# Layer 2's tail and layer 3's tables in six staged groups, degrees broadcast from DRAM, and one loop for long rows instead of three

## The chip, the core and the metric

The kernel runs on one core of one Trainium2 chip. The metric is the device time in microseconds (us). The engines of a core work independently: TensorE (PE; its weight loads are PEld in the profile), VectorE (DVE), ScalarE (ACT), GpSimd (POOL) and SyncE (SP). SP only issues DMAs here. DMAs move data between the core's memory (SBUF) and DRAM.

## The reference

Four graph layers are applied one after the other to x (2708 nodes with 128 features each). The adjacency matrix `adj` is 2708 x 2708; it is sparse (about four entries off the diagonal per row, plus the diagonal). Each layer normalises its input per node, takes its positive part, and adds its result to x.

```python
h = relu(layernorm(x)); x = x + L0(h, adj)   # normalised adjacency @ (h W + b)
h = relu(layernorm(x)); x = x + L1(h, adj)   # attention, 128 groups, adj added to the logits
h = relu(layernorm(x)); x = x + L2(h, adj)
h = relu(layernorm(x)); x = x + L3(h, adj)

def L2(f, adj):
    deg = adj.sum(axis=1, keepdims=True)
    deg = where(deg == 0, 1, deg)
    agg = adj.T @ f / deg
    h = agg @ W_n.T + b_n + f @ W_c.T + b_c
    mu, var = h.mean(axis=0), ((h - h.mean(axis=0)) ** 2).mean(axis=0)
    return relu(gamma * (h - mu) * rsqrt(var + 1e-5) + beta)

def L3(f, adj):
    a, b = f @ w1[:, :128].T, f @ w1[:, 128:].T
    gi = sigmoid(a[None] + b[:, None] + b1) * adj[:, :, None]
    return einsum('ijf,jg->ig', gi, f) @ weight + bias
```

Layer 3 needs, for a node i and each neighbour j, the rows a[j] and f[j]; for the node itself it needs b[i] + b1, and x[i] for the final addition.

## The kernel before

**Tiles.** Nodes lie on the 128 partitions in 22 row tiles (21 full ones and one of 20 rows). Products over all nodes have six column groups of 512 (the last has 148), so a column group is four row tiles. All data are float32. The running x is `x_sb` in SBUF.

**Layer 0** reads the adjacency twice and builds, per node, a sorted list of up to 16 neighbours. It leaves the row sums in `deg` (128 x 22). **Layer 1** takes most of the time; its order of work is written out by hand, and the change does not touch its code. It ends with the last addition to `x_sb` at line 691.

**Layer 2** begins at L1454:

- SP loads the two weights, and these are transposed (L203 to L218). SP loads four columns (L200): two biases, gamma and beta.
- `di`, the inverse degree, is computed on VectorE (L1475 to L1477). It is needed along the free dimension, the same on all partitions (`diB`, 128 x 2708). 22 times, VectorE scales the identity by a column of `di` (L1481), TensorE multiplies a matrix of ones with it (L1483), and ScalarE copies the product to `diB` (L1484).
- SP issues the loads of adjacency row tiles (L1462) into four buffers.
- Two loops (L1498, L1551) stand for inputs on which layer 1's short form is not accurate. Their counts are zero with these inputs, so they are skipped, but all engines take part in the skip, and SP's part waits for the transfers issued earlier.
- `norm_relu` (L220 to L249) makes h and its transpose. The sums (L1578) run over row tiles, six matmuls each, into six banks of PSUM. They are multiplied with `diB` (L1583), put through two linear maps (L1591, L1594), biased (L1597), and VectorE gathers the statistics of the batch norm (L1598 to L1603).
- Per column group, y is normalised on VectorE (L1606), scaled and made positive on ScalarE (L1607), transposed back tile by tile (L1611), and added to `x_sb` (L1612).

**Layer 3** begins at L1617:

- SP loads `w3`, `b3`, `b1` and `w1`. GpSimd clears `more` (L1626). `norm_relu` runs over all 22 tiles: all statistics, one square root (L231), all normalisations (L234, L238), then the transposes (L245, L248).
- Per row tile, TensorE makes a and b together (L1634) and adds b1 through a matmul with a row of ones (L1641). ScalarE copies a (L1645) and h (L1646) into `tab`; VectorE copies b + b1 into `bn` (L1647); SP stores `tab` into the table `gate_d` in DRAM (L1648): one row of 256 values per node, and a row of zeros at the end (L1651).
- Three loops (L1688, L1708, L1752) stand for rows with more neighbours than the lists hold: a count, the rounds, and the addition of `more`. Their counts are zero here. A short computation between the first and the second (L1698 to L1706) yields the number of rounds.
- SP stores `own_d` (b + b1 and x per node) by two calls of `store_rows` (L185 to L189), after these loops in its queue for the second half.
- Per row tile, GpSimd gathers the tile's own rows (L1783) and its neighbours' rows (L1657, 121 gathers in all) by indirect DMAs. The other engines work out the gated sum and the last linear map (L1664 to L1799). GpSimd scatters the result to the output (L1770).

The order within this part comes from the order of the program; each engine works through its own queue in order, and SP's queue holds all the loads and stores above.

Of the kernel before, what the change touches and what calls it, by code (L numbers as in the profile page):

```python
# [9 lines left out]
FP = mybir.dt.float32  # L10
# [6 lines left out]
P = 128  # L17
# [28 lines left out]
def gnn4_kernel(  # L46
# [474 lines left out]


# [929 lines left out]

    with ExitStack() as ph:
# [11 lines left out]
        with tc.tile_pool(name="l2_ps0", bufs=2, space=PSUM) as ps:  # L1465
            wnT = transposed(lp, wk_pool, ps, wn2, "wnT")
            wcT = transposed(lp, wk_pool, ps, wc2, "wcT")
            bias = column_of(lp, bn2, "bn2_sb")
            bc_sb = column_of(lp, bc2, "bc2_sb")
            g_sb = column_of(lp, gamma, "g_sb")  # L1470
            be_sb = column_of(lp, beta, "be_sb")
            nc.vector.tensor_tensor(bias, bias, bc_sb, ALU.add)

            di = lp.tile([P, NT], FP, name="di")
            nc.vector.tensor_scalar(di, deg, 0.0, None, ALU.is_equal)  # L1475
            nc.vector.tensor_tensor(di, di, deg, ALU.add)
            nc.vector.reciprocal(di, di)  # L1477
            diB = lp.tile([P, N], FP, name="diB")
            for t, (r0, sz) in enumerate(rows):
                dg = lp.tile([P, P], FP, name="dg", tag="dg", bufs=2)  # L1480
                nc.vector.tensor_scalar_mul(dg[:sz, :sz], ident[:sz, :sz], di[:sz, t : t + 1])  # L1481
                pd = ps.tile([P, BK], FP, name="d_ps", tag="tr")
                nc.tensor.matmul(pd[:, :sz], ones[:sz], dg[:sz, :sz], start=True, stop=True)  # L1483
                nc.scalar.copy(diB[:, r0 : r0 + sz], pd[:, :sz])  # L1484
# [119 lines left out]
        for c, (c0, cw) in enumerate(cols):  # L1604
            yc = y[:, c0 : c0 + cw]
            nc.vector.tensor_scalar(yc, yc, mv[:, 0:1], rstd, ALU.subtract, ALU.mult)  # L1606
            nc.scalar.activation(yc, yc, AF.Relu, bias=be_sb, scale=g_sb)  # L1607
            for t, (r0, sz) in enumerate(rows):
                if c0 <= r0 < c0 + cw:
                    pt = ps.tile([P, BK], FP, name="y_tr", tag="tr")  # L1610
                    nc.tensor.transpose(pt[:sz, :C], y[:, r0 : r0 + sz], ident)  # L1611
                    nc.vector.tensor_tensor(x_sb[:sz, t], x_sb[:sz, t], pt[:sz, :C], ALU.add)  # L1612


    gate_d = dram.tile([N + 1, 2 * C], FP, name="gate_d")
    own_d = dram.tile([N, 2 * C], FP, name="own_d")
    with ExitStack() as ph:  # L1617
        lp = ph.enter_context(tc.tile_pool(name="l3", bufs=1))
        w3_sb = lp.tile([C, C], FP, name="w3_sb")
        nc.sync.dma_start(w3_sb, w3)  # L1620
        b3_sb = row_of(lp, b3, "b3_sb")
        b1_sb = row_of(lp, b1, "b1_sb")

        bn = lp.tile([P, NT, C], FP, name="bn")
        more = lp.tile([P, NT, C], FP, name="more")
        nc.gpsimd.memset(more, 0.0)  # L1626
        with tc.tile_pool(name="l3w", bufs=1) as wk_pool, tc.tile_pool(
            name="l3_pw", bufs=4, space=PSUM
        ) as ps, tc.tile_pool(name="l3_tab", bufs=4) as tp:
            w1T = transposed(lp, wk_pool, ps, w1, "w1T")  # L1630
            h, hT = norm_relu(lp, ps, "3")
            for t, (r0, sz) in enumerate(rows):
                pw = ps.tile([P, BK], FP, name="ab_ps", tag="tr")
                nc.tensor.matmul(  # L1634
                    pw[:sz, : 2 * C],
                    hT[:, r0 : r0 + sz],
                    w1T.rearrange("p a c -> p (a c)"),
                    start=True,
                    stop=False,
                )  # L1640
                nc.tensor.matmul(  # L1641
                    pw[:sz, C : 2 * C], ones[0:1, :sz], b1_sb, start=False, stop=True
                )
                g = tp.tile([P, 2, C], FP, name="tab")
                nc.scalar.copy(g[:sz, 0], pw[:sz, :C])  # L1645
                nc.scalar.copy(g[:sz, 1], h[:sz, t])  # L1646
                nc.vector.tensor_copy(bn[:sz, t], pw[:sz, C : 2 * C])  # L1647
                nc.sync.dma_start(gate_d[r0 : r0 + sz], g[:sz].rearrange("p a c -> p (a c)"))  # L1648
            z = tp.tile([1, 2 * C], FP, name="tab_z")
            nc.vector.memset(z, 0.0)  # L1650
            nc.sync.dma_start(gate_d[N : N + 1], z)  # L1651
# [27 lines left out]
        with tc.tile_pool(name="l3_more", bufs=2) as mp, tc.tile_pool(  # L1679
# [5 lines left out]
            nc.vector.memset(last, float(N + 1))  # L1685
            nc.vector.memset(count, 0.0)
            adj_flat = adj.rearrange("n m -> (n m)").rearrange("(e o) -> e o", o=1)
            with tc.For_i(0, nc.values_load(ovf, min_val=0, max_val=1)):  # L1688
                ri = mp.tile([P, N], I32, name="key")
# [7 lines left out]
            most = mp.tile([P, 1], FP, name="most")  # L1697
            nc.vector.tensor_reduce(most, count, axis=AX.X, op=ALU.max)  # L1698
            pt = ps.tile([P, BK], FP, name="most_ps", tag="most_ps")
# [139 lines left out]
```

## Time and profile before

| What | us |
|---|---|
| Time before, median of 3 runs | 3235.08 (3232.13 to 3238.72) |
| The profiled execution | 3207.61 |
| Its span, first to last instruction | 3205.8 |
| POOL busy in the span | 2003.3 |
| PE busy | 2615.1 |
| Layer 1's last addition to `x_sb` | begins 2745.79 |
| First matmul of layer 2's sums | begins 2776.29 |
| Batch norm's reciprocal | begins 2892.56 |
| First matmul of layer 3's tables | begins 2920.50 |
| First gather of layer 3 | begins 2979.57 |

A line of the timeline reads: start, time, engine, line of the kernel, operation, output <- inputs, how many in a row, and in brackets the idle time before and what ended it. In the page, a row of digits gives 40 equal slices of the span (9 is 90% busy or more); PEclk is the granted clock of TensorE in tenths.

### The profile page before, as it was taken

How to read it: one execution, taken by the hardware profiler on the slowest of the kernel's cores; microseconds unless marked ns; L12 is line 12 of the kernel's file. 1: busy time of each engine (PE TensorE's matmuls, PEld its weight loads, DVE VectorE, ACT ScalarE, POOL GpSimd, SP SyncE). 2: the span in 40 equal slices, each digit the busy share in tenths (PEclk: the TensorE clock that was granted, in tenths of full speed). 3: DMA queues.
4: the chain of work that ended last, by engine and by line, in shares of the span. 5: the costliest groups of instructions: out<-in, count | busy, mean ns of one | idle time of the engine just before them, and what ended most of it. 6: DMA issues, size and time to landing. Idle time of an engine off the chain costs nothing. (4 is left out here: it accounts for less than half of the span.)

```text
span 3205.8 us, 50411 instructions
## 1 busy us (share of the span) xinstructions
PE 2615.1 (82%) x17997; PEld 2222.6 (69%) x17997; DVE 2182.9 (68%) x5130; ACT 1300.2 (41%) x3165; POOL 2003.3 (62%) x2264
## 2 busy tenths in 40 slices
PE   6477895888889999999999999999888888697144
PEld 4376644887888888878878887878788887443133
DVE  3868744777778888888888887888777676304222
ACT  3576333666644444444444444444433333102010
POOL 0212115666688888888998898989767664000676
PEclk6699897999999999999999999999989999795565
DMA  3463174787733333333343333343355543451332
GB/s 107 175 228 124 66 325 158 238 243 238 210 134 116 131 118 129 137 127 138 118 146 134 138 133 132 137 146 133 84 149 137 125 119 94 165 217 51 102 93 75
DMA packets 309523, 462.53 MB, mean 144 GB/s; under 512 B 153774, under 2 KB 229488, under 8 KB 284178
## 3 DMA queue, kind: packets, MB, share of 16 engines
q1 hardware_dynamic: 277658, 290.28, 28.4%
q0 software_dynamic: 31600, 168.86, 15.4%
q8 instruction: 149, 2.44, 0.3%
q14 instruction: 116, 0.95, 0.1%
HBM read 344.49 MB, written 114.59 MB: 143 GB/s over the span
## 5 line engine op out<-in xcount | busy, mean ns | idle before, releaser
L1302 PE MATMUL g_ps<-mw,fT 128*128 128x128 f32 x5632 | 795.7, 283 | 146.2 <-ACT fT L1292 99.1
L1302 PEld LDWEIGHTS g_ps<-mw,fT 128*128 128x128 f32 x5632 | 707.7, 194 | 265.9 <-ACT fT L1292 155.6
L1292 ACT COPY fT<-f_ps 128x512 f32<-128x512 f32 (+1 forms) x768 | 419.8, 547 | 1114.0 <-PE f_ps L1290 1113.3
L1264 PE MATMUL m_ps<-y,fk 123*128 123x128 f32 (+1 forms) x5632 | 740.0, 276 | 0.0
L1264 PEld LDWEIGHTS m_ps<-y,fk 123*128 123x128 f32 (+1 forms) x5632 | 686.5, 193 | 0.0
L1212 POOL TENSOR_TENSOR y<-bk,raw 128x792 f32<-128x792 f32 x256 | 415.3, 1623 | 386.9 <-ACT y L1245 381.4
L1310 DVE TENSOR_TENSOR z<-g_ps,bq 128x324 f32<-128x324 f32 (+1 forms) x768 | 354.3, 461 | 350.7 <-PE g_ps L1302 350.5
L1290 PE MATMUL f_ps<-ident,fq 128*128 128x128 f32 x2816 | 438.0, 275 | 14.4 <-DVE fq L1209 4.7
L1316 DVE TENSOR_REDUCE o_raw<-z 128x36 f32<-128x324 f32 (+1 forms) x768 | 355.7, 463 | 26.4
L1212 POOL TENSOR_TENSOR fk<-bk,raw 128x352 f32<-128x352 f32 (+1 forms) x384 | 355.8, 949 | 0.1
L1290 PEld LDWEIGHTS f_ps<-ident,fq 128*128 128x128 f32 x2816 | 337.0, 143 | 16.0 <-issue 4.8
L1212 POOL TENSOR_TENSOR fk<-raw,bk 128x352 f32<-128x352 f32 (+1 forms) x512 | 311.0, 636 | 2.9 <-ACT bk L761 2.0
L1209 DVE TENSOR_TENSOR fq<-bq,kq_ps 128x528 f32<-128x528 f32 (+1 forms) x512 | 287.8, 603 | 0.0
L968 POOL TENSOR_TENSOR c_z<-c_kv,c_q 128x1024 f32<-128x1024 f32 (+1 forms) x121 | 284.2, 2348 | 2.0 <-DMA c_kv<-kv_n,srt 1.3
L1009 PE MATMUL v_ps<-c_v,ident 128*128 128x512 f32 (+1 forms) x484 | 232.4, 602 | 15.0 <-ACT c_acc L1024 15.0
L1657 POOL DMA_INDIRECT g<-gate_d,srt x121 | 120.4, 995 | 109.7 <-issue 107.3
L1209 DVE TENSOR_TENSOR fq<-kq_ps,bq 128x352 f32<-128x352 f32 (+1 forms) x512 | 171.5, 377 | 0.0
L155 POOL CAST n_fl<-n_ci 128x40 f32<-128x40 int32 (+1 forms) x22 | 4.8, 216 | 251.7 <-DVE n_ci L138 251.7
L974 DVE TENSOR_REDUCE c_c<-c_z 128x128 f32<-128x1024 f32 (+1 forms) x121 | 147.4, 1218 | 3.5 <-POOL c_z L968 3.1
L992 DVE TENSOR_TENSOR c_v<-c_kv,c_c 128x1024 f32<-128x1024 f32 (+1 forms) x121 | 146.4, 1210 | 0.0
L1009 PEld LDWEIGHTS v_ps<-c_v,ident 128*128 128x128 f32 (+1 forms) x484 | 81.8, 189 | 77.7 <-issue 58.6
L953 POOL DMA_INDIRECT c_kv<-kv_n,srt x121 | 117.5, 971 | 23.4 <-issue 10.4
(301 smaller groups left out, 3670.9 us busy)
## 6 DMA issues: line engine op xcount, KB each, us to landing
a_nat<-in_adj_dram SPq DMA_DIRECT2D x34, 1354.0 KB
raw<-qkv_d SPq DMA_DIRECT2D x128, 275.0 KB
n_raw<-qkv_d SPq DMA_DIRECT2D x128, 275.0 KB
qkv_d<-qkv SPq DMA_DIRECT2D x21, 1600.0 KB
a<-in_adj_dram SPq DMA_DIRECT2D x21, 1354.0 KB
kv_n<-n_kv SPq DMA_DIRECT2D x16, 1408.0 KB
o_g<-o_raw SPq DMA_DIRECT2D x31, 396.0 KB
q_n<-n_q SPq DMA_DIRECT2D x16, 704.0 KB
```

The source lines that it names most:

```text
L968: nc.gpsimd.tensor_tensor(zs[b][:sz], kvs[b][:sz, 0, :, 0], qs[t][:sz], ALU.mult)
L974: nc.vector.reduce_sum(cs[b][:sz], zs.pop(b)[:sz], axis=AX.X)
L992: nc.vector.tensor_tensor(z[:sz], kv[:sz, 0, :, 1].rearrange("p (j c) k -> p j c k", j=2), c.rearrange("p (j c) -> p j c", j=2)[:, :, :, None]
L1009: nc.tensor.matmul(accs[t][:sz, j], ident[:sz, :sz], z[:sz, j].rearrange("p c k -> p (c k)"), start=s0 == 0, stop=s0 == ROOM[t] - 1,)
L1209: nc.vector.tensor_tensor(o, x, y, ALU.mult)
L1212: nc.gpsimd.tensor_tensor(o, x, y, ALU.mult)
L1264: nc.tensor.matmul(pms[d][:, :P], fks[d][:sz, t], ys[d, h][:sz, m * VW * B_ALL : m * VW * B_ALL + P], start=t == 0, stop=t == NT - 1,)
L1290: nc.tensor.transpose(pt[:, m], fqs[d][:, t0 + m], ident)
L1292: nc.scalar.copy(fts[d, c][:, :n], pt[:, :n])
L1302: nc.tensor.matmul(pg[:, m], ft[:, m], mws[d], start=True, stop=True,)
L1310: nc.vector.tensor_tensor(z[:, :n], pg[:, :n, : B_ALL * VW].rearrange("p t (k b) -> p t k b", k=VW), bqs[d % 2][:, t0 : t0 + n, None, :B_A ...
L1316: nc.vector.reduce_sum(ros[g][:, t0 : t0 + n, i], z[:, :n], axis=AX.X,)
```

## The change

It has three parts.

1. `di` is computed right after layer 0 and stored to DRAM as one value per node (`di_d`). Layer 2 loads it with one broadcast DMA into `diB`, in place of the 22 scalings, matmuls and copies. The weights of layer 3 (`w1T`, `w3`, `b3`, and `b1` broadcast to all partitions) are loaded before layer 2. In SP's queue the four columns, `diB` and all adjacency loads now stand behind the two skipped loops of layer 2.
2. From batch norm to the tables, each column group of four row tiles goes through stages: positive part with scale and shift in one ScalarE operation, four transposes, one addition to `x_sb`, statistics, square root, normalisation, positive part, four transposes, four matmuls, copies, and two stores of up to 512 KB, one to `gate_d` and one to `own_d`. A hand-written order interleaves the groups: each round advances every group under way by one stage and begins one more. b1 is added on VectorE; GpSimd copies x into the own rows.
3. The three loops for long rows become one; everything that they need (clearing, reading `own_d` back, the count, the rounds, the addition, the store of x) is inside it.

The diff, cut to its core:

```diff
+    di_d = dram.tile([N, 1], FP, name="di_d")
+    di = keep.tile([P, NT, 1], FP, name="di")
+    nc.vector.tensor_scalar(di[:, :, 0], deg, 0.0, None, ALU.is_equal)
+    nc.vector.tensor_tensor(di[:, :, 0], di[:, :, 0], deg, ALU.add)
+    nc.vector.reciprocal(di[:, :, 0], di[:, :, 0])
+    store_rows(nc.sync, di_d, di)
...
+            w1T = transposed(l3, wk_pool, ps, w1, "w1T")
+            nc.sync.dma_start(w3_sb, w3)
+            nc.sync.dma_start(b3_sb, b3.rearrange("(o c) -> o c", o=1))
+            nc.sync.dma_start(b1B, b1.partition_broadcast(P))
...
-            for t, (r0, sz) in enumerate(rows):
-                dg = lp.tile([P, P], FP, name="dg", tag="dg", bufs=2)
-                nc.vector.tensor_scalar_mul(dg[:sz, :sz], ident[:sz, :sz], di[:sz, t : t + 1])
-                pd = ps.tile([P, BK], FP, name="d_ps", tag="tr")
-                nc.tensor.matmul(pd[:, :sz], ones[:sz], dg[:sz, :sz], start=True, stop=True)
-                nc.scalar.copy(diB[:, r0 : r0 + sz], pd[:, :sz])
+            nc.sync.dma_start(
+                diB, di_d.rearrange("n o -> (o n)").partition_broadcast(P)
+            )
...
+        nc.vector.tensor_tensor(rstd, rstd, g_sb, ALU.mult)
+        nc.vector.tensor_tensor(shift, mv[:, 0:1], rstd, ALU.mult)
+        nc.vector.tensor_tensor(shift, be_sb, shift, ALU.subtract)
...
+            def column(c):
...
+                nc.scalar.activation(yc, yc, AF.Relu, bias=shift, scale=rstd)
+                yield
...
+                for i, sz in part:
+                    nc.tensor.transpose(
+                        pt[:sz, i], yc[:, i * P : i * P + sz], ident
+                    )
...
+                for a, b, sz in parts:
+                    nc.vector.tensor_tensor(xg[:sz, a:b], xg[:sz, a:b], pt[:sz, a:b], ALU.add)
...
+                for i, sz in part:
+                    nc.vector.bn_stats(st3[:sz, i], xg[:sz, i])
+                    nc.vector.bn_aggr(mv3[:sz, i], st3[:sz, i])
+                for a, b, sz in parts:
+                    nc.gpsimd.tensor_copy(own[:sz, a:b, 1], xg[:sz, a:b])
+                yield
...
+                nc.scalar.activation(rs3, mv3[:, :, 1], AF.Sqrt, bias=eps)
+                yield
+                nc.vector.reciprocal(rs3, rs3)
+                for i, sz in part:
+                    nc.vector.tensor_scalar(
+                        tab[:sz, i, 1], xg[:sz, i], mv3[:sz, i, 0:1], rs3[:sz, i : i + 1],
+                        ALU.subtract, ALU.mult,
+                    )
+                yield
+                for a, b, sz in parts:
+                    nc.scalar.activation(tab[:sz, a:b, 1], tab[:sz, a:b, 1], AF.Relu)
+                yield
...
+                nc.scalar.copy(hT3[:, :cw], pt[:, :cw])
+                yield
...
+                for a, b, sz in parts:
+                    nc.scalar.copy(tab[:sz, a:b, 0], pw[:sz, a:b, 0])
+                    nc.vector.tensor_tensor(
+                        own[:sz, a:b, 0],
+                        pw[:sz, a:b, 1],
+                        b1B[:sz, None].to_broadcast([sz, b - a, C]),
+                        ALU.add,
+                    )
...
+                    for dst, src in ((gate_d, tab), (own_d, own)):
+                        nc.sync.dma_start(
...
+            going, todo = [], list(range(NC))
+            while going or todo:
+                if todo:
+                    going.append(column(todo.pop(0)))
+                going = [g for g in going if next(g, "done") != "done"]
...
-            with tc.For_i(0, nc.values_load(ovf, min_val=0, max_val=1)):
...
-        store_rows(nc.sync, own_d[:, :C], bn)
-        store_rows(nc.sync, own_d[:, C:], x_sb)
+                store_rows(nc.sync, own_d[:, C:], x_sb)
```

The removed lines of layer 3 are those named above: `norm_relu` of layer 3, the loop over 22 row tiles with its bias matmuls, copies and stores, and the second and third loop for long rows as loops of their own.

## The prediction

> **What bounds the kernel now.** I read the page first, for the end of the program, and then the timeline from the last addition of layer 1 (2746 us) to the first gather of layer 3 (2980 us), because the diff touches only this stretch, one store before layer 1, and what the gathers read. From the page:
>
> ```profile
> span 3205.8 us, 50411 instructions
> POOL 0212115666688888888998898989767664000676
> PEclk6699897999999999999999999999989999795565
> L1657 POOL DMA_INDIRECT g<-gate_d,srt x121 | 120.4, 995 | 109.7 <-issue 107.3
> ```
>
> Each digit is a slice of 80 us. GpSimd (POOL) has three slices of nothing (2725 to 2965), and then works until the end: those are the gathers of layer 3. They have nothing to overlap with before the tables stand in DRAM. So what counts is when the first gather starts. The timeline gives the marks:
>
> ```profile
> 2745.79 0.28 DVE L691 TENSOR_TENSOR x_sb<-x_sb,c_c 20x128 f32<-20x128 f32 x1 [2.09 <-PE c_c L717]
> 2760.38 0.17 ACT L1484 COPY diB<-d_ps 128x20 f32<-128x20 f32 x1 [0.28 <-PE d_ps L1483]
> 2766.47 1.28 ACT L231 ACT_TABLE_LOAD   x1 [5.91 <-PEq L1551]
> 2776.29 4.08 PE L1578 MATMUL pg<-a,h 128*128 128x512 f32 x8
> 2892.56 0.16 DVE L1603 RECIPROCAL bn_rstd<-bn_rstd 128x1 f32<-128x1 f32 x1 [0.36 <-ACT bn_rstd L1602]
> 2906.27 0.14 POOL L225 MEMSET mv<- 128x44 f32 x1
> 2920.50 1.14 PE L1634 MATMUL ab_ps<-w1T,hT 128*128 128x256 f32 x2
> 2964.16 1.18 SPq L189 DMA_DIRECT2D own_d<-bn  x1
> 2968.94 0.18 DVE L1698 TENSOR_REDUCE most<-count 128x1 f32<-128x22 f32 x1 [7.00 <-SPq L1688]
> 2977.61 1.28 ACT L1667 ACT_TABLE_LOAD   x1 [15.98 <-POOLq L1752]
> 2979.57 1.03 POOL L1657 DMA_INDIRECT g<-gate_d,srt  x1 [73.16 <-issue]
> ```
>
> The reader is to see the chain: layer 1 ends at 2746.1; degrees are spread (diB) until 2760.55; two skipped loops hold every engine until 2766.47; the norm; sums from 2776.29; batch-norm factors ready at 2892.72; then 86.85 us to the first gather. The gathers take the rest, 3205.8 - 2979.57 = 226.2 us. Windows of the table stage and of the transfers:
>
> ```profile
> 2750.00:2756.00 6.00, 5.68 (x21) 4.43 (x20) 2.79 (x10) 2.58 (x10) 0.00 (x0) 0.50 0.95 397
> 2916.00:2918.00 2.00, 1.83 (x8) 1.16 (x7) 2.00 (x9) 2.00 (x9) 0.00 (x0) 0.70 0.00 0
> 2922.00:2960.00 38.00, 38.00 (x83) 20.16 (x83) 5.82 (x20) 9.42 (x41) 0.00 (x0) 0.50 0.20 69
> 2957.00:2958.00 1.00, 1.00 (x4) 0.62 (x3) 0.00 (x0) 0.01 (x1) 0.00 (x0) 0.50 0.37 131
> ```
>
> The columns after the stretch are its length, the busy time of PE, weight load, DVE, ACT, POOL, then the granted TensorE clock, the DMA share and GB/s. The table loop is bound by a TensorE at half clock; its stores need little of the DMA.
>
> **Part 1: degrees and skipped loops in front of layer 2.** The 22 rounds of diagonal, matmul and copy (2747.14 to 2760.55) go. In their place SP stores di before layer 1 and loads 1.39 MB of diB. The loops then wait for the last small load ahead of them. SP issues w3, b3 and b1 at about 0.4 us each from 2745.8; they land near 2749. Add the 5.9 us that the loops took in before (2760.55 to 2766.47): release near 2754.5, 12 earlier. But what stood before the loops on SP now stands behind them: four column loads at 0.43 (1.7 us), diB, and all adjacency loads. In before, tiles 0 and 1 were issued at 2747.66 and landed during the loops. Now diB and tile 0 are issued by 2756.8; they are two tiles' bytes, which took 8.5 us then (2747.66 to about 2756.2, 397 GB/s in the window): tile 0 is there near 2766. The norm alone would allow 2754.5 + 9.8 (2766.47 to 2776.29) = 2764.3. So the first sum is at 2766 instead of 2776.29: **-10.3**. The bounds: -12 if diB is not in the way; if a source row read 128 times comes at 100 GB/s, diB takes 13.5 instead of 3.4 us and the part gives about -1. I take 397, the nearest row. Further tiles need 3.5 us each against 4.54 us of matmul, so sums and y stage (2776.29 to 2892.72) keep their 116.4 us.
>
> The di store goes into SP's queue at about 260 us, between two adjacency loads of the layer before. It has 2708 packets of 4 bytes. The Trainium skill (DMA: Bandwidth & Descriptors, Specifications) says that transfers under 512 bytes are read-modify-writes: a rule against this store. By the page's queue row (277658 packets of q1 in 28.4% of 16 x 3205.8 us) a packet takes 52 ns on average: 2708 x 52 ns / 16 = 9 us of queue. The adjacency loads there are issued three tiles of some 11 us ahead, so over 25 us of slack hides it: **0** by the row. Doubled by the rule (18 us) it is still hidden; uncovered it would cost up to 18.
>
> **Part 2: from the factors to the tables.** Three tiny DVE operations make scale and shift: 0.16 to 0.29 us each, **+0.6**, so the stage starts at T0 = 2893.4 in before's frame. Removed: the full barrier between batch norm, norm and tables (y to 2904.1, POOL's memset of `more` that held back the first aggregate until 2906.45, statistics to 2912.1, h to 2918.6, table loop 2920.5 to 2961.94), 22 bias matmuls, the copies of h, 22 gate stores and four own stores. Instead six groups flow through:
> - DVE per group: add 0.6 (like the 512-wide copies, 0.54 to 0.67), four statistics pairs 1.03 (22 pairs in 5.65 us), four normalisations 1.04 (22 in 5.72 us), reciprocal 0.2, own addition 0.6: 3.4 us; 5.3 groups' worth make 18 us.
> - PE per group: eight transposes at 0.26 (16 took 4.17 us in before's norm stage) are 2.1 us. The table matmul has 256 columns; the sums stream 2708 columns in 4.54 us at clock 1.00, so 0.43 us per tile at full, 0.86 at half clock; the old loop shows 1.22 of modelled time (25.6 us over 21 tiles). At half clock a group is 5.5 to 7 us, all 29 to 37; with 6 to fill and 4 behind the last matmul (copies 0.6, issue 1.2, landing 2) the tables stand at T0 + 39 to 47, say 42.
> - DMA: 2 x 2708 rows of 1 KB are 5.55 MB. The window at 2957 gives 131 GB/s at 0.37, or 354 at full share: 15.7 us. The first own store cannot go before T0 + 17.5: the first own addition stands on DVE behind the additions and statistics of all six groups and four groups' normalisations (2 to fill, 5.3 x 1.63 = 8.7, 4 x 1.24 = 5, itself 0.6, issue 1.2). With 15.7 from there and 2 to land: T0 + 35. This is the floor.
>
> Which clock? In the loop PE was busy for 38.00 of 38.00 us, at 0.50 throughout. The Trainium skill (TensorE: Matmul & The Clock Gate, Part 1) says that about 3.4 us of sustained work opens the clock; by that rule the loop should have run at full clock, and the new stage would be at the floor, T0 + 35 (a median of 3178 in the sum below). The row says half clock, T0 + 42 (3185). The dense transposes at 2916 did raise the clock (0.70), and what went with 0.50 was one-row bias matmuls between weight changes, which are gone. I take **T0 + 37**, nearer to the rule.
>
> GpSimd's copies of 512 elements per group have no row of their own; by the memset of 2816 (2.44 us) and its additions of 792 elements (1623 ns) 0.45 to 1.05 us, six of them under other work: 0, at most +1.
>
> **Part 3: one skipped loop.** After the last landing, before waited 2 us (about 2966.6 to 2968.94) for the first loop, then 1.5 us of round counting, two more loops, and own stores until about 2981. Now one release (+2) and one start of the gather (+2, 2977.6 to 2979.57): first gather at T0 + 41 = 2934.4 against 2979.57, **-45.2**. GpSimd then issues the same 165 gathers and scatters: 226.2 us, **0**, at most 1 either way.
>
> **Sum:** -10.3 - 45.2 = -55.5. The profiled execution took 3207.61 (span 3205.8 and 1.8 around it), so 3152.1 with a span near 3150. The median of the runs shown, 3235.08, lies 27.5 above the profiled one; kept, it gives **3179.6, say 3180**.
>
> **Rivals.**
> A, slow source row or half clock (or both): diB is slow (+9), or the tables stand at T0 + 42 to 46 (+5 to +9). For it: no broadcast load of this size is in the trace, and 0.50 is the clock of every light stage. Against: 397 GB/s for adjacency. Gain 37 to 50: 3185 to 3198.
> B, everything at the floor and sums at 2764.5: clock full, tables at T0 + 35, gain 59: 3176; with an own addition earlier than I see, 3170.
> C, slower than before: the di store. SP's queue is served in order, and adjacency loads stand behind 2708 small writes. To turn a gain of 55 into a loss of over 6.5 it must hold them for 25 + 62 = 87 us: 0.51 us per packet on each of 16 engines, ten times the row. Nothing in the page points there; a price per small write is only not shown.
> D, no change: the stage ends as late as before because stores of three-dimensional form land late, at T0 + 92 (2979.6 - 4, with sums 10.3 earlier). At 5.55 MB that is 76 GB/s from T0 + 17.5 to two before the landing; own_d stores of 512-byte packets reached 290 (2962 to 2966), which speaks against it.
>
> **How the numbers follow.** The sum as told 0.52 (3173 to 3186), A 0.28, B 0.13, C 0.04, D 0.03. No change means within 0.2%, 6.5 us, about what a measurement of this kernel can tell. The first three are faster: 0.93; same 0.03; slower 0.04. The range takes in B's lower part and A with both of its causes: 3166 to 3198.
>
> **What would show it.** First sum at about 2766; factors near 2883; PE clock over 0.7 in the table stage; first gather near 2924, with 226 us behind it; layer 1's last addition still at 2746 within 2 us. If that last mark has moved by more than 10 us, the di store is not hidden. If the sums start after 2770, diB is in the way. If the clock stays at 0.50 and PE is busy throughout, A's second half holds. If the gathers take longer than 230 us, the tables' form matters, which this sum leaves out.

## The result and the profile after

The changed kernel takes 3187.18 us (median of four runs, 3174.70 to 3192.74); the kernel before took 3235.82 beside it (3232.13 to 3238.72). The ratio is 0.9845, with an interval of 0.9813 to 0.9877: faster by 48.6 us, where the forecast was 3180, a gain of 55.5 against the 3235.08 then known. Two later series of runs of the same two programs gave ratios of 0.9829 [0.9798, 0.9859] and 0.9827 [0.9809, 0.9845], 52.5 and 52.1 us.

From the page of the kernel after, the span, GpSimd's row and TensorE's granted clock:

```profile
span 3172.9 us, 49894 instructions
POOL 0211114666688888888989888989876666001775
PEclk6689897999999999999999999999989999797565
```

GpSimd's stretch of nothing is down from three slices to two. The fourth digit from the end, 2855 to 2935 us, holds the table stage, and before it the end of the sums: the clock's digit there is 7, where before had 5 in a slice that lies 30 us later. The marks, from the timeline of the kernel after (the columns are as before; the two stores at 220 us come from the new `di_d`):

```profile
220.94 0.43 SPq L187 DMA_DIRECT2D di_d<-di  x1
221.42 5.09 SPq L189 DMA_DIRECT2D di_d<-di  x1
2742.89 0.28 DVE L698 TENSOR_TENSOR x_sb<-x_sb,c_c 20x128 f32<-20x128 f32 x1 [2.09 <-PE c_c L724]
2751.16 1.28 ACT L231 ACT_TABLE_LOAD   x1 [13.94 <-PEq L1562]
2754.43 0.43 SPq L1493 DMA_DIRECT2D diB<-di_d  x1
2764.93 5.49 PE L1589 MATMUL pg<-a,h 128*128 128x512 f32 x6 [3.04 <-DMA a<-in_adj_dram]
2885.05 0.16 DVE L1614 RECIPROCAL bn_rstd<-bn_rstd 128x1 f32<-128x1 f32 x1 [0.36 <-ACT bn_rstd L1613]
2904.23 0.39 SPq L1699 DMA_DIRECT2D gate_d<-tab  x1
2906.43 0.37 SPq L1699 DMA_DIRECT2D own_d<-own  x1
2924.78 1.28 ACT L1729 ACT_TABLE_LOAD   x1 [7.18 <-SPq L1750]
2925.59 1.05 POOL L1847 DMA_INDIRECT own<-own_d,srt  x1 [20.27 <-issue]
```

The two loops of layer 2 are released 8.0 us after layer 1's last addition has ended (2743.17), and the first sum then waits 3.04 us for its adjacency tile. From the reciprocal to the first gather it is 40.54 us, where it was 87.01. Windows of the same kernel: the loads in front of the sums, the first sums, the rest of the sums, and two overlapping stretches of the table stage (after the stretch: length, PE, weight load, DVE, ACT, POOL, granted clock, DMA share, GB/s):

```profile
2755.00:2764.90 9.90, 2.27 (x8) 1.46 (x8) 9.48 (x48) 5.96 (x23) 0.00 (x0) 0.50 0.95 344
2764.93:2771.00 6.07, 6.07 (x10) 2.86 (x11) 0.83 (x2) 0.00 (x0) 0.00 (x0) 0.50 1.01 428
2771.00:2870.00 99.00, 99.00 (x270) 47.26 (x268) 2.20 (x4) 0.00 (x0) 0.00 (x0) 1.00 0.68 250
2900.70:2920.00 19.30, 12.12 (x59) 8.88 (x58) 10.37 (x36) 7.99 (x19) 1.17 (x4) 1.00 0.75 250
2908.00:2921.00 13.00, 6.85 (x33) 4.64 (x31) 3.52 (x9) 4.33 (x11) 0.00 (x0) 1.00 1.02 340
```

In the table stage the clock is full from 2900.7, and the DMA engines are fully taken from 2908 to 2921: at its end the stage waits for the stores, not for TensorE. A float32 matmul appears as two records in these counts: the 44 matmuls of the old table loop as 88, the 132 of the sums as 264.

One thing in this profile does not belong to the change. The gathers take 247.3 us here (3172.9 - 2925.59). In the two repeats of the same program they take 227.6, about as in the kernel before (226.3). The timeline shows a copy of TensorE's result that comes 19.50 us late:

```profile
3007.91 0.27 ACT L1858 COPY sup<-sup_ps 128x128 f32<-128x128 f32 x1 [19.50 <-remote]
```

"remote" marks a release for which the profile names no instruction; ScalarE's table of waits for this kernel shows five of them:

```profile
ACT sup L1858 <- remote: 64.5, 5, 20.6
ACT sup L1858 <- PE sup_ps L1854: 31.7, 12, 4.9
```

(Columns: total us, times, longest.) So the account of the change below uses the first repeat, `after_again`, whose span is 3153.1.

### The profile page after: what moved, and what is told of

Read it like the earlier page. It is cut to its first block, busy times and chain, and to the rows that moved or that the text cites. A ratio compares the mean times of both kernels' runs of the same rounds, so it can differ in the third digit from the quotient of the medians.

```text
span 3172.9 us, 49894 instructions
## 1 busy us (share of the span) xinstructions
PE 2576.5 (81%) x17908; PEld 2205.8 (70%) x17908; DVE 2169.3 (68%) x5067; ACT 1291.2 (41%) x3102; POOL 2004.8 (63%) x2275
## 3 DMA queue, kind: packets, MB, share of 16 engines
q0 software_dynamic: 31600, 168.86, 15.5%
## 5 line engine op out<-in xcount | busy, mean ns | idle before, releaser
L960 POOL DMA_INDIRECT c_kv<-kv_n,srt x121 | 117.5, 971 | 23.4 <-issue 11.2
```

## The experiments

The runs after the first result were made in three series, each with the kernel before beside it: its medians are 3212.26 us (beside after_again and undo1_diag to undo3_loops), 3211.45 (beside before_again, dib_late, warm_dib_late and old_no_b1) and 3213.38 (beside the rest). Each ratio is against the median of its own series. "Reciprocal to gather" is the table stage with the skipped loops behind it. "Layer 1 to reciprocal" starts at the end of the last addition to `x_sb`. "One" in the table marks a single run, for which there is no interval. The profiled executions:

| Kernel | Layer 1 ends | Layer 1 to reciprocal | Reciprocal to gather | Gathers | Time: median, or one run | Ratio [interval] |
|---|---|---|---|---|---|---|
| before | 2746.07 | 146.5 | 87.01 | 226.3 | 3207.61, one | |
| before_again | 2758.32 | 144.3 | 87.08 | 227.0 | 3218.51, one | |
| after_again | 2743.22 | 141.7 | 40.54 | 227.6 | 3159.75 | 0.9829 [0.9798, 0.9859] |
| after_third | 2756.62 | 140.9 | 40.79 | 227.6 | 3161.30 | 0.9827 [0.9809, 0.9845] |
| undo1_diag | 2758.72 | 144.4 | 40.33 | 226.6 | 3172.24 | 0.9857 [0.9824, 0.9890] |
| undo2_tables | 2755.68 | 140.6 | 75.71 | 226.3 | 3199.53 | 0.9945 [0.9926, 0.9963] |
| undo3_loops | 2747.52 | 142.2 | 51.74 | 227.1 | 3173.29 | 0.9871 [0.9841, 0.9902] |
| old_no_b1 | 2745.07 | 142.3 | 48.76 | 227.3 | 3165.25, one | |
| old_full_rows | 2743.42 | 142.5 | 52.48 | 226.9 | 3167.08, one | |
| staged_b1rows | 2747.05 | 139.9 | 68.72 | 226.9 | 3184.39, one | |
| dib_late | 2757.53 | 137.3 | 40.81 | 226.9 | 3161.30 | 0.9830 [0.9800, 0.9860] |
| warm_dib_late | 2749.07 | 142.7 | 40.84 | 227.3 | 3157.23 | 0.9820 [0.9794, 0.9847] |
| early_own | 2744.46 | 138.5 | 38.81 | 226.6 | 3156.75 | 0.9823 [0.9799, 0.9846] |

The first column moves by up to 13 us between executions of one program (see the last section), and the medians carry that along. What a stage is worth is therefore read from the marks, and the medians serve as a bound. The marks have noise of their own. Reciprocal to gather lies between 40.33 and 40.84 us in the six profiles whose code is the same there. Layer 1 to reciprocal lies between 139.9 and 142.5 us in the seven of this table with the unaltered head of the kernel after.

### The kernel after again, and each part undone

The kernel after, unaltered:

> The changed kernel once more, unaltered. In its first profile the first gather began at 2925.6 us and the gather stage took 247.3 us instead of 226.2, with TensorE's results up to 24 us late there. Theory 1 (the lateness belongs to one execution, not to the program): this profile has a gather stage of 226 to 232 us and no late results. Theory 2 (it belongs to the changed program): 240 to 255 us again, with results late by more than 5 us at least three times. By both the first gather is at 2920 to 2930, and the median of the timed runs is 3180 to 3193.

The gathers are back at 227.6 us. ScalarE's waits in this profile have no line of the remote kind any more:

```profile
ACT z L1729 <- DVE z L1726: 174.6, 22, 25.5
ACT sup L1858 <- PE sup_ps L1854: 20.7, 7, 4.5
```

The late results thus do not belong to the program; what made them late is open. The median, expected at 3180 to 3193, came at 3159.75: the runs of the first series were slower, before and after alike, and the record does not show why.

**Part 1 undone**: `di` is spread by 22 diagonals again; the store of `di_d` and the early loads of weights stay.

```diff
-            nc.sync.dma_start(
-                diB, di_d.rearrange("n o -> (o n)").partition_broadcast(P)
-            )
+            for t, (r0, sz) in enumerate(rows):
+                dg = lp.tile([P, P], FP, name="dg", tag="dg", bufs=2)
+                nc.vector.tensor_scalar_mul(dg[:sz, :sz], ident[:sz, :sz], di[:sz, t])
+                pd = ps.tile([P, BK], FP, name="d_ps", tag="tr")
+                nc.tensor.matmul(pd[:, :sz], ones[:sz], dg[:sz, :sz], start=True, stop=True)
+                nc.scalar.copy(diB[:, r0 : r0 + sz], pd[:, :sz])
```

> The changed kernel with part 1 undone: diB is made again by 22 scalings, matmuls and copies, and with that adjacency tiles 0 and 1 go before the skipped loops again; the store of di stays. Prediction's sum: the first sum matmul begins 10 us later than in the changed kernel, counted from the last addition of layer 1 (30 us behind it instead of 21.8), everything after it is unchanged, and the median rises by 8 to 10 us. Rival (the earlier loops gained nothing since adjacency tile 0 came late): at most 3 us.

Layer 1 to reciprocal takes 144.4 us instead of 141.7: the part is worth 2.6 us, and not the 8 to 10 of the expectation. Against the profile of before it is 4.8 (146.5), against its repeat 2.6 (144.3). The first sum comes 27.90 us after layer 1 with the part undone, and 21.61 with it; but the sums take 105.20 us instead of 102.75, and so more than a third of those 6.3 us is gone by the time they end. The medians differ by 12.5 us, which would seem to confirm the 8 to 10. But the profiled execution of `undo1_diag` ended layer 1 15.5 us later than that of `after_again`, at code that the edit does not touch, so the median cannot be put down to this part.

**Part 2 undone**: the stage by groups is replaced by before's y loop, norm over all tiles, and table loop; single loop and part 1 stay.

```diff
-            going, todo = [], list(range(NC))
-            while going or todo:
...
+            h, hT = norm_relu(lp, ps, "3")
+            for t, (r0, sz) in enumerate(rows):
+                pw = ps.tile([P, BK], FP, name="ab_ps", tag="tr")
...
+                nc.tensor.matmul(
+                    pw[:sz, C : 2 * C], ones[0:1, :sz], b1B[0:1], start=False, stop=True
+                )
...
+        store_rows(nc.sync, own_d[:, :C], bn)
+        store_rows(nc.sync, own_d[:, C:], x_sb)
```

> The changed kernel with part 2 undone: y is normalised, transposed and added, norm and tables follow as before, with one store of 128 KB per tile, and own rows stored afterwards; part 1 and the single loop stay. Prediction's sum: from the batch norm's reciprocal to the first gather 36 us more than in the changed kernel (about 76 instead of 40.5), median up by 33 to 38. If the late TensorE results come from the tables' stores or from the memory that the groups leave behind, the gather stage is 226 us here, and the median rises by only 12 to 17.

Reciprocal to gather is 75.71 us instead of 40.54: part 2 is worth 35.2 us (36 expected). The median rises by 39.8 us (33 to 38 expected).

**Part 3 undone**: three loops for long rows instead of one, with the clearing of `more` outside of them as in before.

```diff
+            nc.gpsimd.memset(more, 0.0)
+            nc.vector.memset(last, float(N + 1))
+            nc.vector.memset(count, 0.0)
...
-                rounds = nc.values_load(n_i, min_val=0, max_val=N // 8 + 1)
-                with tc.For_i(0, rounds):
+            rounds = nc.values_load(n_i, min_val=0, max_val=N // 8 + 1)
+            with tc.For_i(0, rounds):
...
+            with tc.For_i(0, nc.values_load(ovf, min_val=0, max_val=1)):
```

> The changed kernel with part 3 undone: three skipped loops with the count of rounds between them in place of one. Prediction's sum: landing of the last table store to first gather 4 us plus 1.5 for the count plus two more loops of 2.5 to 3: 6 to 8 us later, median up by 6 to 8. If the late TensorE results come from the single loop (the engines meet less often, or the program lies elsewhere), the gather stage is 226 us here and the median falls by 10 to 15.

51.74 us instead of 40.54: part 3 is worth 11.2 us. The timeline of `undo3_loops` shows what is in it:

```profile
2928.04 2.44 POOL L1748 MEMSET more<- 128x2816 f32 x1 [17.82 <-SPq L1753]
2930.87 0.18 DVE L1763 TENSOR_REDUCE most<-count 128x1 f32<-128x22 f32 x1 [2.67 <-POOLq L1753]
2941.45 1.05 POOL L1848 DMA_INDIRECT own<-own_d,srt  x1 [10.96 <-issue]
```

GpSimd clears `more` only after the release of the first loop, and the round count on VectorE starts when it has done so: 2.8 us (2928.04 to 2930.87). The remaining 8.4 us are the count and two more skipped loops, and lie somewhat above the 6 to 8 that were expected of them. In before the clearing lay earlier, ahead of the norm, so this kernel overstates the part by it. Parts 2 and 3 add up: 35.2 + 11.2 = 46.4, of 87.01 - 40.54 = 46.5.

### What in part 2 saved the time

The old table loop runs at half clock with TensorE busy throughout. Three kernels, each with a single run, ask whether this comes from the one-row bias matmuls or from the loop's form. The first drops them from `undo2_tables` (`b1` is added on VectorE):

```diff
-                    stop=False,
+                    stop=True,
                 )
-                nc.tensor.matmul(
-                    pw[:sz, C : 2 * C], ones[0:1, :sz], b1B[0:1], start=False, stop=True
-                )
...
-                nc.vector.tensor_copy(bn[:sz, t], pw[:sz, C : 2 * C])
+                nc.vector.tensor_tensor(bn[:sz, t], pw[:sz, C : 2 * C], b1B[:sz], ALU.add)
```

> The kernel with part 2 undone, in which only the bias changes: b1 is added by VectorE while it copies b, and the 22 matmuls with a row of ones go. If those one-row passes are what kept the clock of the old table loop at 0.50 although TensorE was busy all the time, the clock comes to 1.00 within 7 us of the loop's start, and the loop takes 17 to 24 us for 22 tiles instead of 41. If something else keeps it (the loop's weight changes, its small steps), the clock stays at 0.50 and the loop takes 25 to 30 us.

The second keeps as many matmuls with as many columns, but over 128 rows: `b1Z` is zero except for its first row, which holds b1.

```diff
-                    pw[:sz, C : 2 * C], ones[0:1, :sz], b1B[0:1], start=False, stop=True
+                    pw[:sz, C : 2 * C], ones[:, :sz], b1Z, start=False, stop=True
```

> The kernel with part 2 undone, in which only the shape of the bias matmul changes: it runs over 128 rows (b1 in the first, zeros in the others) instead of one. Instructions, columns and weight changes are the same. If it is the single row that keeps the clock at 0.50, the clock comes to 1.00 within 7 us of the loop's start and a tile takes 0.9 to 1.1 us instead of 1.87: the reciprocal to the first gather is 55 to 62 us. If it is the number of passes or the changes of weights, the clock stays at 0.50 and it is 75 to 77 us as before.

The third puts the one-row matmuls into the new stages:

```diff
+                    nc.tensor.matmul(
+                        pw[:sz, i, 1], ones[0:1, :sz], b1B[0:1], start=False, stop=True
+                    )
```

> The changed kernel with only the bias turned back: b1 comes from a matmul with a row of ones after each table matmul, and VectorE copies instead of adding. If those passes keep the clock down, it stays at 0.50 through the whole table stage and the reciprocal to the first gather is 47 to 56 us instead of 40.5. If they only cost their own time (22 x 0.43 us at full clock, beside a DMA that is the bound), the clock comes to 1.00 after some 15 us and it is 40.5 to 43 us.

Windows over the table loop of `undo2_tables`, of `old_full_rows` and of `old_no_b1`, and over the table stage of `staged_b1rows` (columns as above):

```profile
2922.60:2963.40 40.80, 40.80 (x89) 21.21 (x88) 7.09 (x24) 9.73 (x42) 0.00 (x0) 0.50 0.20 67
```

```profile
2912.20:2928.10 15.90, 15.90 (x89) 13.98 (x88) 6.53 (x22) 8.62 (x37) 0.00 (x0) 0.92 0.46 156
```

```profile
2913.60:2926.00 12.40, 12.39 (x45) 7.98 (x44) 6.59 (x22) 8.69 (x38) 0.00 (x0) 0.90 0.54 180
```

```profile
2900.00:2945.00 45.00, 42.62 (x102) 23.50 (x100) 12.01 (x46) 7.83 (x19) 1.82 (x6) 0.50 0.28 94
```

The first two have the same number of TensorE instructions. Only the rows of the bias matmul differ, and the loop takes 15.9 instead of 40.8 us, at a clock of 0.92 instead of 0.50. So it is the one row, not the count of matmuls, nor the mere change of weights between them. Most of what the 128 rows hold is zero, so it is not the values either. All three kernels missed their expectations by size: the loop of `old_no_b1` takes 12.4 us (17 to 24 expected), `old_full_rows` has 52.48 us from reciprocal to gather (55 to 62), and `staged_b1rows`, which keeps 0.50 as well, has 68.72 (47 to 56) where the stages without one-row matmuls have 40.54.

The half clock is not all that the one row costs. Both kernels below run at 0.50 in these lines, the second only until 2914.60:

```profile
2942.43 0.50 PEld L1642 LDWEIGHTS ab_ps<-b1B,ones 1*128 1x128 f32 x2 [0.65 <-issue]
2942.44 0.79 PE L1642 MATMUL ab_ps<-b1B,ones 1*128 1x128 f32 x2
2944.31 0.79 PE L1642 MATMUL ab_ps<-b1B,ones 1*128 1x128 f32 x2
```

```profile
2912.76 0.77 PEld L1645 LDWEIGHTS ab_ps<-b1Z,ones 128*128 128x128 f32 x2
2913.18 0.64 PE L1645 MATMUL ab_ps<-b1Z,ones 128*128 128x128 f32 x2
2914.47 0.47 PE L1645 MATMUL ab_ps<-b1Z,ones 128*128 128x128 f32 x2
```

In `undo2_tables` the weight load of the bias matmul begins together with it, and a tile takes 1.87 us (a bias matmul begins at 2942.44, the next at 2944.31). In `old_full_rows` the weight load begins 0.42 us ahead of the matmul, and a tile takes 1.29 us (2913.18 to 2914.47). The difference of 0.58 us, 22 times, is about 13 us at the same clock. So, by estimate from these lines, about half of the 25 us between the two loops is weight loading that no longer overlaps, and the other half is the clock.

Of part 2's 35.2 us, 26.95 therefore go to the bias matmuls (75.71 - 48.76; 23.2 of them by the row count alone, 75.71 - 52.48), and 8.2 to the staging (48.76 - 40.54). With the one-row matmuls kept, staging gives 7.0 (75.71 - 68.72).

### The head of layer 2

`diB` is needed only at the end of the sums, but is loaded ahead of adjacency tile 0. In `dib_late` its load stands behind the first four tiles:

```diff
-            nc.sync.dma_start(
-                diB, di_d.rearrange("n o -> (o n)").partition_broadcast(P)
-            )
...
         for t in range(min(4, NT)):
             rows_of_adj2(t)
+        nc.sync.dma_start(
+            diB, di_d.rearrange("n o -> (o n)").partition_broadcast(P)
+        )
```

> The changed kernel with one load moved: diB, which is first read 100 us later, is issued behind the four adjacency tiles instead of ahead of them. If the first sum waits for adjacency tile 0 as the changed kernel's profile shows (3.0 us of waiting), it begins 18 to 19.5 us after the last addition of layer 1 instead of 21.6. If the norm sets it, it stays at 21 or above. The sums still take 104.5 to 106 us by the theory that TensorE's clock, not the loads, makes them longer than 102.6; if the loads did, they take longer still by as much as they start earlier. Median down by 1 to 3 us at most.

The first sum comes 18.22 us after layer 1 instead of 21.61, and layer 1 to reciprocal takes 137.3 instead of 141.7 us. So 3.4 us of the sum's start were diB's bytes. (The median, 3161.30 us, does not show the 4.4: it equals that of `after_third`.) `warm_dib_late` adds eight matmuls ahead of the norm, whose result nothing reads, to have the clock open when the sums begin:

```diff
+        wp = ps.tile([P, BK], FP, name="warm", tag="tr")
+        for i in range(8):
+            nc.tensor.matmul(
+                wp, ident, x_sb[:, 0:4].rearrange("p t c -> p (t c)"), start=True, stop=True
+            )
```

> The same with eight additional matmuls of 128x512 on data at hand, whose result nobody reads, on TensorE's idle time before the norm's transposes. If the sums are slower in the changed kernel only because TensorE comes out of an idle stretch at half clock (0.50 until 2771), the sums take 102.5 to 103.5 us now, and from layer 1's last addition to the batch norm's reciprocal it is 136 to 138.5 us instead of 141.7. If the clock is not the cause, 104.5 to 106 us again, and nothing is gained over the version without them.

The sums take 103.8 us instead of 105.0 (102.5 to 103.5 expected); but the fillers hold back the norm's transposes, the first sum comes at 24.87, and the stretch takes 142.7 us (136 to 138.5 expected): worse than without them. In the same series the kernel before was profiled again, unaltered:

> The kernel before, once more, unaltered. Its profile so far had a gather stage of 226.3 us with no TensorE result late, while its timed runs beside the first profile of the changed kernel lay 27.5 us above it. If that distance is a property of the chip that a job gets and sits in the gather stage, then a time near 3235 goes with a gather stage of 245 to 255 us and late results here, and a time near 3210 with 226 to 228 us and none.

Its table stage is that of the first profile (87.08 us), its gathers take 227.0 us with nothing late, and its layer 1 ends 12.3 us later. Its time of 3218.51 us lies near neither of the two that were expected, so the distance of 27.5 us did not come back and stays without a cause. The last kernel has `dib_late`, four fillers, and the x half of the own rows stored straight from `x_sb`, right after the addition, instead of after a copy on GpSimd together with b:

```diff
+                        nc.sync.dma_start(
+                            own_d[n0 : n0 + (b - a - 1) * P + sz, C:].rearrange(
+                                "(t p) k -> p t k", p=sz
+                            ),
+                            xg[:sz, a:b],
+                        )
...
-                for a, b, sz in parts:
-                    nc.gpsimd.tensor_copy(own[:sz, a:b, 1], xg[:sz, a:b])
```

> The changed kernel with three small edits: diB behind the adjacency tiles; four additional matmuls on TensorE's idle time ahead of layer 2's sums, whose result nobody reads; and x's half of the own rows stored from x_sb as soon as it is added, so that GpSimd's copies go. If adjacency tile 0 and the cold clock cost what the runs so far show, layer 1's last addition to the batch norm's reciprocal is 134 to 136 us instead of 141.7. If the table stage ends where the DMA ends (share 1.02 from 2908 to 2921 in the changed kernel), the reciprocal to the first gather is 37.5 to 39.5 us instead of 40.5; if computing ends it, 40.5 as before. Together 7 to 10 us by the marks; in the median 4 to 10 below the changed kernel's, unless layer 1 hides it.

And, in the same series, the kernel after a third time:

> The changed kernel a third time, unaltered, as the neighbour of the next run. By the theory that the late TensorE results of its first profile belong to one execution: gather stage 226 to 229 us, none late. One VectorE multiplication in layer 1 took 14.25 to 14.27 us in four of the ten profiles so far and 2.56 or less in the others, in different programs and in two executions of the kernel before: it takes one of these two times here, and layer 1's last addition is near 2743 or near 2755 accordingly.

Timeline of `early_own`, from the fillers to the first gather:

```profile
2757.57 5.93 PE L1582 MATMUL warm<-x_sb,ident 128*128 128x512 f32 x8 [12.30 <-DVE ln_st L228]
2764.20 3.60 PE L1594 MATMUL pg<-a,h 128*128 128x512 f32 x8
2882.93 0.16 DVE L1619 RECIPROCAL bn_rstd<-bn_rstd 128x1 f32<-128x1 f32 x1 [0.36 <-ACT bn_rstd L1618]
2921.74 1.03 POOL L1859 DMA_INDIRECT own<-own_d,srt  x1 [168.91 <-issue]
```

Reciprocal to gather falls from 40.5 to 38.8 us: the stores start earlier and the stage ends earlier, as was expected (37.5 to 39.5) of a stage that its stores bound. Layer 1 to gather takes 177.3 us, 5.0 less than in `after_again`. Layer 1 to reciprocal is 138.5 us, where 134 to 136 were expected. The fillers begin 5 us after the loops' release and in front of the transposes: the first sum comes at 19.74, 1.5 us later than in dib_late, and the sums take 103.76 us, 1.3 less, so in sum the fillers bring nothing. The whole is 5.0 where 7 to 10 were expected. The medians of `early_own` and `after_third` (3156.75 and 3161.30) cannot be told apart: 0.9823 [0.9799, 0.9846] and 0.9827 [0.9809, 0.9845].

## Why the prediction was right

From the profile of before to that of `after_again` the span goes from 3205.8 to 3153.1, by 52.7 us. By the prediction's own steps:

| Step | Predicted | Measured |
|---|---|---|
| Layer 1's end | 0 | -2.9 |
| Layer 1's end to the first sum | -10.3 | -8.6 |
| Sums and y stage | 0 | +3.9 |
| Reciprocal to the first gather (parts 2 and 3) | -45.2 | -46.5 |
| Gathers | 0 | +1.4 |
| Sum | -55.5 | -52.7 |

**Part 1, first half: right in its steps, too large in its sum.** The loops' release was put at 8.4 us after layer 1 and came at 8.0; diB and tile 0 were put at 8.5 us from issue and took 10, at 344 GB/s instead of 397. The bound of 100 GB/s for a row read 128 times was far off. Of the 8.6 us, 2.5 belong to the one profile of before: its first sum comes 30.23 us after layer 1, in `before_again` 27.75 and in `undo1_diag` 27.90. The 22 rounds of diagonal and matmul, over 14.48 us from layer 1's end, had a clock of 0.63 in the first and 0.92 in the second:

```profile
2746.07:2760.55 14.48, 11.86 (x44) 9.10 (x44) 7.04 (x28) 5.61 (x22) 0.03 (x1) 0.63 0.52 194
```

```profile
2758.32:2772.80 14.48, 7.98 (x44) 6.14 (x44) 6.89 (x29) 5.61 (x22) 0.04 (x1) 0.92 0.53 195
```

Against the repeat the step is 6.1 us, not 10.3.

**Part 1, second half: "sums and y stage keep their 116.4 us" failed.** They took 3.9 us more, 120.1 in place of 116.3, and halved the part: 4.7 of 10.3 us are left, by `undo1_diag` 2.6. In before, the sums followed closely on the norm's transposes, and a window over their first 6.01 us has 23 records at a mean clock of 0.92:

```profile
2776.29:2782.30 6.01, 6.01 (x23) 3.24 (x23) 5.19 (x15) 3.05 (x12) 0.00 (x0) 0.92 0.03 6
```

In the kernel after, TensorE has little to do ahead of the sums (2.27 of 9.90 us), has waited 3.04 us for tile 0 and starts at 0.50: 10 records in the first 6.07 us (second row of the windows after). The loss is complete within these first matmuls: up to the last row tile the sums take 97.8 us in before and 100.4 in the kernel after, 2.6 apart. In `early_own`, whose clock is 1.00 from the start, it is 97.3. But its sums as a whole take 103.76 us, since the clock falls again before they end. The last row tile has only 20 rows (matmuls of 20x512), from 2861.49 on in this profile. Windows of its first sums, of its last row tile until the clock falls, and of the rest of that tile:

```profile
2764.20:2768.00 3.80, 3.80 (x14) 1.84 (x13) 2.60 (x8) 1.75 (x7) 0.00 (x0) 1.00 0.99 419
2861.49:2864.50 3.01, 3.01 (x8) 1.40 (x8) 0.00 (x0) 0.00 (x0) 0.00 (x0) 1.00 0.00 0
2864.50:2867.96 3.46, 3.46 (x6) 1.33 (x4) 0.00 (x0) 0.00 (x0) 0.00 (x0) 0.50 0.00 0
```

The clock also accounts for the other 1.2 us, between the last sum and the reciprocal. This stretch takes 13.7 us in before and 14.9 in the kernel after, with as many records of TensorE, which are busy 1.23 us longer, and the same work on VectorE and ScalarE:

```profile
2878.86:2892.56 13.70, 11.04 (x25) 5.00 (x24) 7.30 (x14) 4.00 (x7) 0.00 (x0) 0.88 0.00 1
```

```profile
2870.12:2885.05 14.93, 12.27 (x25) 5.44 (x24) 7.30 (x13) 4.00 (x7) 0.00 (x0) 0.78 0.01 1
```

A mean of 0.88 over 13.70 us is 3.3 us at half clock, 0.78 over 14.93 is 6.6. The stretch takes 13.5 to 13.7 us in the four profiles in which its mean clock is 0.86 or more, and 14.9 to 15.0 in the three at 0.77 or 0.78. So the term that was put at nothing is the state of the clock, at both ends of the sums.

**The di store, 0: right.** SP has 5.09 us of issue for it at 221 (put at about 260), and layer 1 ends at 2743.2, not later than before's 2746.1. For the rule of the Trainium skill ("DMA: Bandwidth & Descriptors", Specifications) on transfers under 512 bytes, these runs show no price on the path, though layer 1's end moves by some 6 us between the nine undisturbed profiles (last section), so a small one could not be seen; the doubling to 18 us was the prediction's own estimate, which no run here tests. Rival C falls with it.

**Part 2: right in sum, and the choice of clock too; the mechanism only in part.** The first store, to `gate_d`, is issued at T0 + 18.4 and the first own store at T0 + 20.6 (predicted 17.5; T0 is 2885.8 here). The last stores end at about 2923.7, T0 + 38 (predicted 37). The clock is 0.50 until 2900.7 and then 1.00. From 2908 to 2921 the DMA engines are full at 340 GB/s (predicted 354), so the floor that the prediction named is the bound. The 37 was not summed but chosen between 35 and 42, so its closeness is in part luck. The prediction put the half clock down to "one-row bias matmuls between weight changes": `old_full_rows` confirms the one-row half of that, and shows that as many weight changes with 128 rows do not hold the clock down. What the prediction did not say is that the row count alone would bring 23 us, about half of it through weight loads that stand in the matmuls' way. It credited the gain to the removed barrier and to the stages; those bring 7 to 8 us. The half-clock part of rival A and rival D fall; B's floor was missed by about 3 us.

**Part 3: right.** Behind the landing, 2 + 2 us were predicted for release and gather; from about 2923.7 to 2925.59 it is 1.9. Against before's 13 (2966.6 to 2979.57) the prediction's frame makes 9 of this part, the measured one 11; undoing it costs 11.2, or 8.4 without the clearing of `more`.

**The median.** 27.5 us between profile and median of before were carried over. In the later series before's median is 3211.45 to 3213.38, about 5 above its profile: those 27.5 us were no property of the kernel. That the level of 3180 came out rests on both kernels being slow together in the first series. The profile after was 12.5 us under its own median, with 20 us of late results in it. Of the 7.2 us by which 3180 lies under the measured 3187.18, the marks explain 2.8 (55.5 - 52.7), of which part 1's sums are the largest term; the rest is within the interval of the ratio, which reaches from 40 to 60 us of gain.

## What to carry to other kernels

A bias added by a matmul with a row of ones is no small change beside a light chain of matmuls: 22 of them kept TensorE at half clock, kept its weight loads from overlapping, and took 23 to 28 us here; add the bias in the copy out of PSUM. When a load moves in front of another, look at what the engine behind it does meanwhile: here TensorE, busy for 2.3 of 9.9 us and then waiting, began the sums at half clock. Read a part's worth from the marks around it, since an end-to-end median can carry a shift of 12 us from elsewhere.

## What the hardware showed that was not expected

**Matmuls that use few rows do not hold the clock.** The Trainium skill ("TensorE: Matmul & The Clock Gate", Part 1) has the clock open after some 3.4 us of sustained work. Here 40.8 us at 40.80 busy stayed at 0.50 as long as every second matmul had one row; with 128 rows the mean was 0.92. The measurement decides: "busy" in the profile is not the work that the clock follows. That loop also has the weight loads that do not overlap, so it cannot tell few rows from gaps. The 20-row matmuls at the end of the sums have no such gaps: they follow each other every 0.43 us at full clock, as those of 128 rows do, and yet the clock falls 3.0 to 4.2 us after the first of them, while they still run, in nine of the fourteen profiles. This points to the rows; no run gave that tile more of them. With 128 rows the page's figure is near: in the nine profiles that begin the sums at half clock, it opens 3.2 to 6.1 us after the first sum.

**A multiplication on VectorE that takes 14 us.** In layer 1, once near 2320 us, the same instruction takes 2.56 us in nine profiled executions and 14.25 to 14.29 us in five (before_again, undo1_diag, undo2_tables, dib_late, after_third). Timelines of `after_again`, of `after_third`, the same program, and of `before_again`:

```profile
2319.06 2.56 DVE L1110 TENSOR_TENSOR r_more<-r_raw,r_rs 128x704 f32<-128x704 f32 x1
2320.82 1.50 POOL L1219 TENSOR_TENSOR fk<-bk,raw 128x352 f32<-128x352 f32 x1
```

```profile
2320.70 14.29 DVE L1110 TENSOR_TENSOR r_more<-r_raw,r_rs 128x704 f32<-128x704 f32 x1
```

```profile
2322.04 14.26 DVE L1103 TENSOR_TENSOR r_more<-r_raw,r_rs 128x704 f32<-128x704 f32 x1
2322.00 1.86 POOL L1096 TENSOR_TENSOR r_both<-r_both 128x792 f32<-128x792 f32 x1
2323.82 0.84 POOL L1212 TENSOR_TENSOR fk<-bk,raw 128x352 f32<-128x352 f32 x1
...
2332.81 2.75 POOL L1212 TENSOR_TENSOR fk<-bk,raw 128x528 f32<-128x528 f32 x3
```

GpSimd works back to back from 2322.00 to 2335.56 in `before_again`, and the multiplication ends 0.7 us later. GpSimd has the same instructions in all fourteen profiles. In the nine its second one (`fk`) takes 1.5 us, and the multiplication has ended by then; in the five it takes 0.84, and VectorE gets no turn until GpSimd's row of instructions is over. Layer 1 ends at 2743 to 2749 in the nine and at 2756 to 2759 in the five. This fits the port pair that VectorE and GpSimd share, a lock held for an instruction (the Trainium skill, "SBUF — State Buffer", Terms), if the lock can pass VectorE by for several GpSimd instructions in a row. That is an argument; no run here took GpSimd's work away, and what decides between the two outcomes is open: in both, VectorE's instruction begins 38 to 64 ns after GpSimd's.

**Waits of up to 20.6 us for TensorE's results**, in the first profile of the kernel after alone, in five waits of the remote kind. Whether they belong to that execution or to its whole series, whose other runs were slower still, is open.
